# A four-layer graph network: late parameters by the loads' queue, masks in three stages, attention's input by quarters within the first loop, loops and slots by six places

## The chip, the cores and the metric

The kernel runs on one core of a Trainium2 chip. The metric is the device time of one execution in microseconds (us). The core's engines work side by side, each through its own instruction stream: TensorE (PE; its weight loads are listed apart as PEld), VectorE (DVE), ScalarE (ACT), GpSimd (POOL) and SyncE (SP), which here issues nearly all DMA transfers. The median before is 4793.08 us of three runs (4787.59 to 4794.63).

## The reference, cut to what matters

Eight samples of 2048 nodes with 128 features, one adjacency matrix of 2048 x 2048 shared by all, about 3% of it ones. Every layer normalises its input and applies relu, and its result is added to x.

```python
for layer in (0, 1, 2, 3):
    h = relu(layernorm(x))
    x = x + f[layer](h, adj)

# 0: h = layernorm(((w + 1) * h + b) @ W) * gamma + beta
#    e = leaky_relu(s1[i] + s2[j]); att = softmax(where(adj > 0, e, -9e15))
#    f = elu(att @ h + h)
# 1: four heads of 32: softmax(where(adj, q @ k.T / sqrt(32), -inf)) @ v @ Wo + bo
# 2: relu(h @ Wself + bself + (adj @ h / degree) @ Wneigh + bneigh)
# 3: h = h @ W.T; e = leaky_relu(s[i] + d[j]); f = softmax(where(adj, e, -1e9)) @ h
```

## The kernel before

**Tiles.** A sample's x lies in four chunks `xb[g]` of 128 x 4 x 128 (512 nodes each). Nodes go in 16 tiles of 128. The order of PE, DVE, ACT and POOL is the order in which Python emits the instructions; SP's order and the place of every tile in its pool are chosen by the framework. `later(f)` puts a reader of a PSUM tile off until more work has been issued, `settle` emits what was put off. `Steps.skewed(n, stages)` emits stage s of item i in step i + s, so that the items run through the stages one behind another; `merged` lays two lists side by side by weight.

**Parameters (L187 to L262).** All weight matrices and rows come by ACT's own DMA queue, nineteen transfers, in the order of the code: `w0`, seven more matrices (L200 to L206), five rows broadcast to 128 partitions, and then six small transfers into `rows` (node weights, node biases, the two attention vectors). `rows` is turned by PE (`pcol`) into columns which layer 0 needs.

**The head (L1142 to L1229).** `mask_steps` has one step per tile of 128 rows of adj: `one` loads 1 MB (L1144), compares into 0/1 (`nb01`, bf16, on DVE, L1146), raises it to the mask of attention (`pmt`, int8, with row sums, on ACT, L1149), stores it (L1152), transposes its 16 squares on PE in two halves of eight (L1162), copies one half into `mst` (fp8) by DVE (L1165) and one by ACT (L1167), and at the end of a group of three or two tiles stores `mst` to `mg_all` (L1169). `degrees` (L1176) computes reciprocal degrees and the bias rows of layer 2 (`hbs`, L1191). The first ten tiles are merged with `layer0_ahead(0)`, which prepares layer 0 of the first sample (load of h L587, normalise, `weigh` on POOL L592, transposes and projection, normalise, `scale` and `shift` on POOL L618 and L621). `gat_rows` then sends the row of s2 through memory, broadcast to all partitions. The other six tiles and `degrees` are merged into the first 35% of the first layer-0 loop, and `before_attention(0)` follows the loop.

**The loops of layers 0 and 3 (`gat_loop`, L452 ff.).** Nodes in six groups, `GROUPS`, of 3, 3, 3, 3, 2, 2 tiles. A step handles two tiles of neighbours jp: `leaky` (ACT, L508), `lowered` (DVE, L514), `exps` (ACT, L518), `masked` (DVE, L523), `product` (PE, L534, six or four times two matmuls into `gacc`). The stages of one step belong to different jp, one step apart. At the end of a group `ended` (L549) reads `gacc` and `closed` adds. `ahead(k + 1)` prepares the next group in between: `maxi` (`gat_maximum`, L445, DVE, reads a mask `pmg` of 256 KB loaded for it), `shifts` and `spread`, which sends the rows `ab` through memory by SP.

**Attention.** `before_attention(b)` (L682 ff.) normalises a chunk, turns it (L694), projects q and k (`pqk`) and v (`pv`), and stores them to memory, from where `heads` and `queries` load them. The 256 blocks (sample, 256 queries, head) run as a stream of sub-steps, twelve to a block, six to each half `t`: sub-step 0 issues `scores` (PE, L932), half of `values` and `exponentials` (ACT, L956) of the half before; 1 the other values; 2 `masked_scores` (DVE, L948); 3 and 4 the eight-fold transposes T0 and T1 of the block before (PE, L968); 4 and 5 the copies C0 and C1 (ACT, L973). `pending` carries the end of a group of four heads: `po`, `rT`, `pwo` and the addition to x.

**Laying the layers side by side.** While attention of sample b runs, layers 2 and 3 of sample b - 1 and layer 0 of sample b + 1 are laid between the sub-steps. `work` lays by weight. For samples 1 to 6 the loops are laid by `locked` instead: one loop step to three sub-steps. `PLACES` and `PLACES_B` say behind which of the three each stage goes, for the first half of the six sub-steps (A) and the second (B). In the last part of a sample `locked` also lays `tail` (`before_attention(b + 1)` and `layer0_ahead(b + 2)`) over the first 60% of the steps.

Of the kernel before, what the change touches and what calls it, by code (L numbers as in the profile page):

```python
# [31 lines left out]
def gnn_kernel(  # L32
# [94 lines left out]
    def later(f):  # L127
        unread.append([f])
        return unread[-1]
# [70 lines left out]
    wq = load_w("wq", W_q)  # L200
    wk = load_w("wk", W_k)
    wv = load_w("wv", W_v)
    wo = load_w("wo", W_o)
    wself = load_w("wself", W_self)
    wneigh = load_w("wneigh", W_neigh)
    w3 = load_w("w3", W3)  # L206
    gam = load_row("gam", ln_g)
    bet = load_row("bet", ln_b)
    bo1 = load_row("bo1", b_o)
    bself = load_row("bself", b_self)  # L210
    bneigh = load_row("bneigh", b_neigh)

    nc.vector.tensor_scalar(bo1, bo1, -1.0, None, ALU.add)
# [42 lines left out]
    pw3 = psum("pw3", (P, P))  # L256
    nc.tensor.transpose(pw3, w3, ident)
    nc.vector.tensor_copy(w3T[:, 0:P], pw3)

    pwa = psum("pwa", (P, 2))  # L260
    nc.tensor.matmul(pwa, w3, a12_3, start=True, stop=True)
    nc.vector.tensor_copy(w3T[:, P : P + 2], pwa)  # L262
# [318 lines left out]
    def layer0_ahead(b):  # L581
# [3 lines left out]
        def load(g):  # L585
            h[g] = new(hp3, "h", "h", (P, 4, P))
            nc.sync.dma_start(out=h[g], in_=x_chunk(b, g))  # L587

        def weigh(g):
            for k in range(4):  # L590
                t = 4 * g + k
                nc.gpsimd.tensor_scalar(  # L592
                    h[g][:, k, :], h[g][:, k, :], nw1[:, t : t + 1], nb[:, t : t + 1],
                    ALU.mult, ALU.add,
                )
# [21 lines left out]
        def scale(g):  # L617
            nc.gpsimd.tensor_tensor(hv(g), hv(g), bc_mid(gam, 4), ALU.mult)  # L618

        def shift(g):  # L620
            nc.gpsimd.tensor_tensor(hv(g), hv(g), bc_mid(bet, 4), ALU.add)  # L621
# [54 lines left out]
    def before_attention(b):  # L676
# [34 lines left out]
        def project_v(g):  # L711
# [16 lines left out]
        steps = Steps()  # L728
        steps.skewed(
            G,  # L730
            norm_stages(lambda g: xb[g], hdst) + [turned, project, project_v],
            1.0,
        )
        return steps
# [324 lines left out]
    SUB = 12  # L1059
    state = {"exp": None, "old": None, "older": None, "ahead": None, "pair": None, "ao": None}  # L1060

    def block_steps(n):
# [36 lines left out]

        def sub(t, s):  # L1100
            def go():
                if t == 0 and s == 0:
                    begin()
                old, older = state["old"], state["older"]
                if s == 0 and n < len(blocks):
                    scores(blk, t)
                if s < 2:
                    if t == 0 and real("older"):
                        values(older, 2 + s)
                    if t == 1 and real("old"):  # L1110
                        values(old, s)
                if s == 0 and state["exp"]:
                    exponentials(*state["exp"])
                    state["exp"] = None
                if s == 2 and n < len(blocks):
                    masked_scores(blk, t)
                    state["exp"] = (blk, t)
                if s in (3, 4) and real("old"):
                    turned(old, 2 * t + s - 3)
                if s in (4, 5) and real("old"):  # L1120
                    copied(old, 2 * t + s - 4)
# [15 lines left out]

    def mask_steps():
        steps = Steps()
        st = {}  # L1140

        def one(it):  # L1142
            at = new(ep, "e", "adj", (P, N), I32)
            nc.sync.dma_start(out=at, in_=adj[it * P : (it + 1) * P, :])  # L1144
            nb01 = new(op, "dump", "nb01", (P, N), BF16)
            nc.vector.tensor_scalar(nb01, at, 0.0, None, ALU.is_gt)  # L1146
            pmt = new(mp, "pm", "pmt", (P, N), I8)

            nc.scalar.activation(  # L1149
                pmt, nb01, AF.Copy, scale=-64.0, bias=64.0, accum_out=nsum[:, it : it + 1]  # L1150
            )
            nc.sync.dma_start(out=pm_all[it], in_=pmt)  # L1152
            gk = next(k for k, (i, n) in enumerate(GROUPS) if i <= it < i + n)
            i0, n = GROUPS[gk]
            if it == i0:
                st["m"] = new(ep, "e", "mst", (P, T, n * P), FP8)
            c = (it - i0) * P
            for g in range(T // 8):
                pt = psum("pmask", (P, 8, P), BF16)
                for k in range(8):  # L1160
                    jt = g * 8 + k
                    nc.tensor.transpose(pt[:, k, :], nb01[:, jt * P : (jt + 1) * P], ident_bf)  # L1162
                dst = st["m"][:, g * 8 : (g + 1) * 8, c : c + P]
                if g == 0:
                    nc.vector.tensor_copy(dst, pt, saturate=False)  # L1165
                else:
                    nc.scalar.copy(dst, pt, saturate=False)  # L1167
            if it == i0 + n - 1:
                nc.sync.dma_start(out=mg_all[gk], in_=st["m"])  # L1169

        for it in range(T):
            steps.add(5.0, lambda it=it: one(it))
# [45 lines left out]
    with tc.manual_schedule(engines=ENGINES):  # L1218
        st0, pre = layer0_ahead(0)
# [180 lines left out]
```

## Time and profile before

| what | value |
| --- | --- |
| median of three runs | 4793.08 us |
| profiled execution | 4792.7 us |
| its span, first to last instruction | 4790.8 us |
| PE busy | 4126.7 us, 86% |
| DVE busy | 3906.3 us, 82% |
| ACT busy | 3613.4 us, 75% |
| POOL busy | 454.9 us, 9% |
| mean granted clock of TensorE | 0.943 |
| moved by DMA | 423 MB, 88 GB/s over the span |

The page is one profiled execution. Busy shares are means over stages: in the row of slices each digit is the busy share of a fortieth of the span (120 us) in tenths, 9 being 90% or more, and PEclk the clock that TensorE was granted. A group line names line, engine, operation, destination and sources with their shapes and the count; behind the bars stand the busy sum in us and the mean of one in ns, then the idle time of the engine just before them and what ended most of it. A timeline line begins with the time from the start of the span and the duration. A line of waits names who waited, for whom, and sum in us, count and longest. Three groups fill much of the body: attention's copy of transposed tiles (ACT L973, 1007 us), its masked scores (DVE L948, 1212 us) and the loops' product (PE L534, 1122 us).

### The profile page before, as it was taken

How to read it: one execution, taken by the hardware profiler on the slowest of the kernel's cores; microseconds unless marked ns; L12 is line 12 of the kernel's file. 1: busy time of each engine (PE TensorE's matmuls, PEld its weight loads, DVE VectorE, ACT ScalarE, POOL GpSimd, SP SyncE). 2: the span in 40 equal slices, each digit the busy share in tenths (PEclk: the TensorE clock that was granted, in tenths of full speed). 3: DMA queues.
4: the chain of work that ended last, by engine and by line, in shares of the span. 5: the costliest groups of instructions: out<-in, count | busy, mean ns of one | idle time of the engine just before them, and what ended most of it. 6: DMA issues, size and time to landing. Idle time of an engine off the chain costs nothing.

```text
span 4790.8 us, 87729 instructions
## 1 busy us (share of the span) xinstructions
PE 4126.7 (86%) x33290; PEld 2842.0 (59%) x33290; DVE 3906.3 (82%) x8337; ACT 3613.4 (75%) x5121; POOL 454.9 (9%) x413
## 2 busy tenths in 40 slices
PE   2569998998898988998799988989889998989976
PEld 2535665576656666575665766567665666646645
DVE  5967777888978898788988889788987898658849
ACT  4637986698868988598885978689885988749926
POOL 2020002001200031001300012000310000000000
PEclk7768999999999999999999999999999999999988
DMA  8432113323232232412233132322324123222122
GB/s 268 137 91 57 46 40 114 95 59 102 79 123 62 68 103 76 133 51 86 82 103 102 59 101 77 120 66 68 103 74 134 50 73 99 79 77 61 52 89 76
DMA packets 308354, 423.34 MB, mean 88 GB/s; under 512 B 61222, under 2 KB 177628, under 8 KB 303836
## 3 DMA queue, kind: packets, MB, share of 16 engines
q1 hardware_dynamic: 305984, 416.85, 28.7%
q8 instruction: 263, 4.31, 0.4%
q14 instruction: 159, 1.30, 0.1%
q10 hardware_dynamic: 1948, 0.87, 0.1%
HBM read 365.78 MB, written 55.98 MB: 88 GB/s over the span
## 4 chain that ended last, share of the span: by engine, by line
PE 33%; DVE 29%; ACT 28%; issue 6%; DMA 3%; SPq 1%; ACTq 0%; DVEq 0%
ACT e L956 8%; ACT eT L973 8%; PE pt L968 7%; DVE e L948 7%; PE pagg L787 7%; PE gacc L534 6%; ACT ge L508 6%; PE sc L932 5%; DVE dump L445 4%; DVE ge L514 4%; DVE ge L523 4%; PE acc L983 3%; ACT ge L518 3%; PE ph L393 1%; DVE ln_s L336 1%
## 5 line engine op out<-in xcount | busy, mean ns | idle before, releaser
L973 ACT COPY eT<-pt 128x1024 f32<-128x1024 f32 x1024 | 1007.3, 1012 | 568.7 <-PE pt L968 566.0
L948 DVE CUSTOM_DVE_ANT_0 e<-sc,pm 128x1024 f32<-128x1024 f32 x1024 | 1211.5, 1220 | 212.0 <-PE sc L932 207.0
L534 PE MATMUL gacc<-haug,ge 128*128 128x129 f32 x8192 | 1122.4, 288 | 178.3 <-DVE ge L523 94.6
L968 PE MATMUL pt<-ident,e 128*128 128x128 f32 x8192 | 1079.0, 282 | 159.0 <-DVE amh L948 74.1
L534 PEld LDWEIGHTS gacc<-haug,ge 128*128 128x128 f32 x8192 | 1016.7, 199 | 335.5 <-issue 264.8
L968 PEld LDWEIGHTS pt<-ident,e 128*128 128x128 f32 x8192 | 943.5, 145 | 285.1 <-DVE amh L948 101.7
L956 ACT ACTIVATE e<-e,amn 128x2048 f32<-128x2048 f32 x512 | 1031.4, 2014 | 29.6 <-DVE amn L952 29.6
L508 ACT ACTIVATE ge<-ab,s 128x384 f32<-128x384 f32 (+1 forms) x1536 | 803.5, 577 | 121.5 <-DMA ab<-rowd 74.0
L932 PE MATMUL sc<-ks,qr 32*128 32x512 f32 x4096 | 786.9, 660 | 71.5 <-ACT eT L973 46.2
L514 DVE TENSOR_TENSOR ge<-ge,ab 128x768 f32<-128x768 f32 (+1 forms) x768 | 683.8, 890 | 52.5 <-ACT ge L508 46.2
L523 DVE SCALAR_TENSOR_TENSOR ge<-mg,ge 128x768 f32<-128x768 fp8e4 (+1 forms) x768 | 666.6, 868 | 24.7 <-ACT ge L518 23.2
L518 ACT ACTIVATE ge<-ge 128x768 f32<-128x768 f32 (+1 forms) x768 | 595.1, 776 | 118.0 <-DVE ge L514 115.9
L445 DVE CUSTOM_DVE_ANT_0 dump<-s2b,pmg 128x2048 bf16<-128x2048 f32 x256 | 585.5, 2287 | 39.4 <-DMA s2b<-rowd 32.2
L983 PE MATMUL acc<-eT,vv 128*32 128x256 f32 x8192 | 587.6, 397 | 2.6 <-ACT eT L973 2.6
L346 POOL TENSOR_TENSOR ln_r<-ln_ve,neg_half 128x4 f32<-128x4 f32 x160 | 207.2, 1295 | 3868.4 <-DVE ln_ve L340 3623.7
L983 PEld LDWEIGHTS acc<-eT,vv 128*32 128x32 f32 x8192 | 206.8, 111 | 508.7 <-issue 428.0
L932 PEld LDWEIGHTS sc<-ks,qr 32*128 32x128 f32 x4096 | 241.6, 189 | 263.9 <-ACT eT L973 142.5
L787 PE MATMUL pagg<-mt,hm 128*128 128x512 fp8e4 x1536 | 356.1, 381 | 9.3 <-DVE agT L805 9.3
L787 PEld LDWEIGHTS <-hm 128*128 128x128 bf16 x1536 | 147.2, 98 | 183.6 <-issue 30.7
L379 PE MATMUL ptr<-ident,h 128*128 128x128 f32 x512 | 92.3, 307 | 54.2 <-DVE amh L948 19.3
L1036 DVE TENSOR_TENSOR aoT<-po,rT 128x256 f32<-128x256 f32 x64 | 27.1, 424 | 127.6 <-ACT rT L1031 127.5
L379 PEld LDWEIGHTS ptr<-ident,h 128*128 128x128 f32 x512 | 66.8, 155 | 85.5 <-issue 28.8
(126 smaller groups left out, 2601.8 us busy)
## 6 DMA issues: line engine op xcount, KB each, us to landing
pmg<-pm_all SPq DMA_DIRECT2D x256, 256.0 KB
mg<-mg_all SPq DMA_DIRECT2D x128, 384.0 KB
pm<-pm_all SPq DMA_DIRECT2D x128, 256.0 KB
qr<-qd SPq DMA_DIRECT2D x1024, 32.0 KB
mt<-mt_all SPq DMA_DIRECT2D x64, 512.0 KB
ab<-rowd SPq DMA_DIRECT2D x64, 384.0 KB
adj<-in_adj_dram SPq DMA_DIRECT2D x16, 1024.0 KB
s2b<-rowd SPq DMA_DIRECT2D x16, 1024.0 KB
```

The costliest lines, as they stand in the source:

```text
L445: nc.vector.tensor_tensor_reduce(dump, st["s2b"], pm, UP, HIGHEST, ALU.add, ALU.min, st["mn"][:, it : it + 1])
L508: nc.scalar.activation(e[:, c, :], gr[k]["s1"], AF.Prelu, bias=st["s2"][:, j : j + 1], alpha=ALPHA)
L514: nc.vector.tensor_tensor(e, e, bc_mid(gr[k]["m"], 2), ALU.subtract)
L523: nc.vector.scalar_tensor_tensor(e, mt, BIG, e, ALU.mult, ALU.min)
L534: nc.tensor.matmul(gr[k]["acc"][:, q, :], e[:, c, q * P : (q + 1) * P], st["haug"][:, j, :], start=(j == 0 and q == 0), stop=(j == T - 1), ...
L787: nc.tensor.matmul(st["pa"], st["hm"][:, j, s, :], st["mt", g, j // 8][:, j % 8, :], start=(j == 0 and s == 0), stop=(j == T - 1 and s == ...
L932: nc.tensor.matmul(blk["sc"][g // 2][:, (g % 2) * 512 : (g % 2 + 1) * 512], blk["q"][r, t * P : (t + 1) * P], ks_t[b, hh][r, :], start=Tru ...
L948: nc.vector.tensor_tensor_reduce(e[:, c], blk["sc"][h], pm[:, c], UP, HIGHEST, ALU.add, ALU.min, mh[:, h : h + 1])
L956: nc.scalar.activation(blk["e"][t], blk["e"][t], AF.Exp, scale=-1.0, bias=blk["mn"][:, t : t + 1], accum_out=blk["ao"]["sum"][:, t, blk["h ...
L968: nc.tensor.transpose(pt[:, c, t, :], blk["e"][t][:, j * P : (j + 1) * P], ident)
L973: nc.scalar.copy(eT, blk.pop(("pt", w)).rearrange("p c t n -> p c (t n)"))
L983: nc.tensor.matmul(pair["acc"][g * HD : (g + 1) * HD, blk["hh"] % 2, :], vv_t[blk["b"], blk["hh"]][:, j, :], blk["eT"][w][:, g, :], start= ...
```

## The change

Parameters: ten of the thirteen matrices and rows are issued by SP, behind four loads of h and four of adj. What is computed of `w3` and `bo1` moves to `late_constants`, which runs behind `gat_rows`.

Masks: the step of a tile is split into three stages that run skewed, with the loads of adj four tiles ahead. The transposes of a tile go into one PSUM tile and ACT copies it whole; DVE copies none. `mst` and `nb01` take slots of other pools. Eleven entries of the skewed list are merged with layer 0's preparation, three more run before the loop, the rest (last stores and `degrees`) in its first tenth. `weigh`, `scale` and `shift` of sample 0 run on DVE.

Attention's input: `before_attention` can be emitted for some of the four chunks. For sample 0 chunk g goes into the loop, one step of it per loop step, once group 1, 2, 3 or 5 has closed.

Loops and slots: `ORDER` lists what each of the six sub-steps emits; T1 moves from sub-step 4 to 3. `locked` has six places to a loop step instead of three, one before and one behind each of the three sub-steps (odd ones are behind: 1, 3, 5 are the old 0, 1, 2). `product` goes from the second to the third sub-step, `maxi` of the second half from behind the second to before the first, `ended` of the first half from the second to the first. The share of `tail` falls from 0.6 to 0.55.

```diff
-    wq = load_w("wq", W_q)
...
-    bneigh = load_row("bneigh", b_neigh)
-
-    nc.vector.tensor_scalar(bo1, bo1, -1.0, None, ALU.add)
+    late = [("wq", W_q), ("wk", W_k), ("wv", W_v), ("wo", W_o), ("wself", W_self)]
+    late += [("wneigh", W_neigh), ("w3", W3), ("bo1", b_o), ("bself", b_self), ("bneigh", b_neigh)]
...
+    def load_late():
+        for t, ap in late.values():
+            nc.sync.dma_start(out=t, in_=ap if len(ap.shape) == 2 else ap.partition_broadcast(P))
...
-    def layer0_ahead(b):
+    def layer0_ahead(b, eng=nc.gpsimd):
...
+    ORDER = [
+        ["S", "V0", "exp"],
+        ["V1"],
+        ["ttr"],
+        ["T0", "T1"],
+        ["C0"],
+        ["C1"],
+    ]
...
+    def neighbours(it):
+
+        nb01[it] = new(tp, "eT", "nb01", (P, N), BF16)
+        nc.vector.tensor_scalar(nb01[it], adj_t.pop(it), 0.0, None, ALU.is_gt)
+        load_adj(it + 4)
+
+    def mask_turned(it):
+        gk, i0, n = group_of(it)
+        if not mst:
+            mst["all"] = new(bp, "big", "mst", (P, 2, T, 3 * P), FP8)
+        mst[gk] = mst["all"][:, gk % 2, :, 0 : n * P]
+        c = (it - i0) * P
+        pt = psum("pmask", (P, T, P), BF16)
+        for jt in range(T):
+            nc.tensor.transpose(pt[:, jt, :], nb01[it][:, jt * P : (jt + 1) * P], ident_bf)
+        later(lambda: nc.scalar.copy(mst[gk][:, :, c : c + P], pt, saturate=False))
...
+        steps.skewed(T, [neighbours, turned_raised, mask_stored], 5.0)
...
-        early, late = Steps(masks_all[:10]), Steps(masks_all[10:])
-        rest = merged(early, pre)
-        rest.add(1.0, lambda: gat_rows(st0))
-        rest.extend(merged(layer0_loop(0, st0, True), late, 0.35))
-        rest.extend(before_attention(0))
+        n = 11
+        rest = merged(pre, Steps(masks_all[:n]))
+        rest.add(1.0, lambda: gat_rows(st0), lambda: load_x(0))
+        rest.add(1.0, late_constants)
         run(rest)
+        loop = layer0_loop(0, st0, True)
+        quarters, queue, others = before_attention(0), [], masks_all[n:]
+        start = len(loop) - 9 * len(GROUPS) - 6
+        for _ in range(3):
+            run([others.pop(0)])
...
+            for g, group in enumerate((1, 2, 3, 5)):
+                if k == start + 9 * group + 13:
+                    queue.extend(quarters([g]))
+            if queue:
+                run([queue.pop(0)])
+        run(others + queue)
...
-        PLACES = {'product': 1, 'masked': 0, 'exps': 1, 'lowered': 0, 'leaky': 1, 'ended': 1, 'closed': 0, 'maxi': 0, 'other': 2}
-        PLACES_B = {'product': 1, 'masked': 0, 'exps': 0, 'lowered': 1, 'leaky': 0, 'ended': 1, 'closed': 1, 'maxi': 1, 'other': 2}
+        PLACES_A = {
+            "product": 5, "masked": 1, "exps": 3, "lowered": 1, "leaky": 3,
+            "ended": 1, "closed": 1, "maxi": 1, "other": 5,
+        }
+        PLACES_B = {
+            "product": 5, "masked": 1, "exps": 1, "lowered": 3, "leaky": 1,
+            "ended": 3, "closed": 3, "maxi": 0, "other": 5,
+        }
...
-                    locked(both[n:], tail, 0.6)
+                    locked(both[n:], tail, 0.55)
```

## The prediction

> **What bounds the kernel now.** I read the slices first, then the busy time by stage, then the timeline at the ends of the stages, then the groups and waits inside them.
>
> ```profile
> PE   2569998998898988998799988989889998989976
> DVE  5967777888978898788988889788987898658849
> ACT  4637986698868988598885978689885988749926
> PEclk7768999999999999999999999999999999999988
> ```
> A slice is 120 us. The first three slices show PE at 2, 5 and 6 tenths, and DVE and ACT hardly better: nothing is full there. From the fourth on PE stands at 8 or 9, ACT and DVE close behind, and the three change places as the fullest. So the kernel has a head that waits and a long body that is packed. The change touches both.
>
> The head by stages (columns: stretch, us, busy of PE, PEld, DVE, ACT, POOL with counts, clock, DMA share, GB/s), and one stretch of the body for comparison:
>
> ```profile
> 0.00:97.30 97.30, 26.89 (x217) 23.33 (x217) 48.67 (x149) 40.92 (x55) 31.36 (x46) 0.83 0.81 273
> 97.30:117.70 20.40, 3.78 (x32) 3.25 (x32) 14.37 (x16) 5.86 (x7) 0.00 (x0) 0.50 0.78 246
> 117.70:258.30 140.60, 84.33 (x577) 78.30 (x577) 131.31 (x223) 94.22 (x162) 0.00 (x0) 0.80 0.42 131
> 258.30:287.20 28.90, 19.54 (x72) 11.83 (x72) 11.80 (x62) 8.43 (x16) 10.15 (x9) 0.74 0.49 152
> 2212.00:2401.00 189.00, 151.96 (x1228) 109.87 (x1228) 173.85 (x398) 147.80 (x216) 53.28 (x41) 0.94 0.30 89
> ```
> Masks and projections (0 to 97.3) have no engine above half and DMA at 81%: the chain adj, compare, transposes, two copies, store runs nearly one tile after the other. The first layer-0 loop (117.7 to 258.3) has DVE busy 93%: DVE is its pace. In the 28.9 us before the first attention block every engine is under 70%: a chain of dependent steps. The last row, seventeen half-blocks in which attention's next input is laid beside the loop, has DVE at 92%; 15.1 us of it are idle.
>
> ```profile
> 15.33 1.28 ACT L1149 ACT_TABLE_LOAD   x1 [15.33 <-DMA rows<-in_L_gnn_node_bias_dram]
> 117.66 2.13 ACT L508 ACTIVATE ge<-ab,s 128x384 f32<-128x384 f32 x4 [5.12 <-DMA ab<-rowd]
> 287.23 1.23 DVE L948 CUSTOM_DVE_ANT_0 e<-sc,pm 128x1024 f32<-128x1024 f32 x1 [11.78 <-PE sc L932]
> ```
> Start, duration, and in brackets the wait with its releaser: ACT's first work, the first step of the loop, the first masked scores. All further numbers are counted to these three.
>
> **The change part by part.** The sum is made against the profiled execution: 4792.7 us, span 4790.8, which is within 0.4 us of the median of the runs (4793.08), so no correction is needed.
>
> *Parameters.* ACT's first work waits for a row that was queued behind the ten parameters. Ten issues of about 0.45 us leave ACT (4.5), and SP takes them after four h and four adj loads. Here the Trainium skill, "DMA: Bandwidth & Descriptors", section on issuing engines not being separate DMA queues, speaks against more: several issuers share the 16 engines and save issue time only. By that rule 4.5 us at most are won, no transfer time. The trace's row lets ACT start 15.3 late with DMA at 81%, which agrees; I take 3.3, start near 12, as the small rows now also land beside the h and adj loads.
>
> *Masks in three stages.*
> ```profile
> L1165 DVE CAST mst<-pmask x16: 1224/1225/1225, 23.3 to 160.9; 128x1024 fp8e4<-128x1024 bf16 x16
> L1167 ACT CAST mst<-pmask x16: 987/1012/1012, 24.1 to 161.8; 128x1024 fp8e4<-128x1024 bf16 x16
> ```
> Two half copies per tile, DVE 1.225 and ACT 1.01, become one ACT copy of twice the width. "ScalarE: Activation LUTs", section Rules for kernel authors, gives such simple work to VectorE, up to three times faster in bf16. By the rule DVE should have kept both halves, and the move would cost 16 times at least 1.2 us on ACT for nothing. The row says ACT is faster on this copy, 1.01 to 1.225, so I follow the row: one ACT copy at 1.9 (between one 1.01 and two of them, less one fixed start; upper end 2.02). ACT then carries per tile 1.91 (raise) + 0.19 (sum) + 1.9 = 4.0, times 16 = 64, and 11.3 for layer 0's projections, about 5 of gaps: from 12 to 92. DVE and POOL are relieved (weigh, scale and shift of sample 0 go from POOL to DVE, which has room: 48.7 of 97.3). Then the rows of s2, the first maxima and the shifts: 20.4 us now; the next three mask tiles lie beside it, and the maxima's loads stand on SP behind the stores of masks 11 to 13. I let the loop begin at **104** (was 117.66). Bounds: DMA must move some 31 MB before it (16.8 adj, 8.4 mask stores, 5.5 h, x, parameters and rows), 283 GB/s is the best 60 us I read: 110; without that limit 98. Gain 13.7 (6 to 20).
>
> *The first loop.*
> ```profile
> L1165 DVE CAST mst<-pmask 128x1024 fp8e4<-128x1024 bf16 x4 | 4.9, 1225 | 3.8 <-PE pmask L1162 3.8
> L1146 DVE TENSOR_SCALAR nb<-adj 128x2048 bf16<-128x2048 int32 x4 | 4.9, 1220 | 0.0
> L1191 DVE SCALAR_TENSOR_TENSOR hbs<-bneigh,has,bself 128x128 f32<-128x128 f32 x16 | 4.3, 332 | 0.0
> ```
> These are DVE's mask groups inside the loop: count, busy and mean ns, then idle before and its releaser. They leave it: 4.9 + 4.9 + 3.8 of waiting + 4.3 and 0.7 of small steps = 18.6. Three quarters of before_attention come in: DVE's statistics and normalising, about 2.5 each (0.86 + 0.36 + 0.17 + 1.1) = 7.5. DVE is the pace, so 140.6 - 11.1 = **129.5**: the loop ends at 233. ACT rises from 94 by three turns and projections, about 12, still under 129; that hides it. If ACT's copies stood between two leaky steps on the path, 5 come back.
>
> *Input by quarters.* After the loop, 28.9 us now: four skewed quarters and the loads of q, k, v. One quarter stays: statistics 1.6, root 1.0 on POOL, apply 1.1, turn 2, projection 2, copies 2, two DMA trips of about 2 to 3 and the scores 2.6: about 17. First masked scores at **250** (was 287.2); so far 37. From 287 to 340 the first blocks have waits of up to 15 us; k, v and the second sample's h come earlier, I take 3. Head: **-40** (20 if the early stage is bound by DMA and the quarters delay the loop, 52 if neither).
>
> *Loops by six places.* In steady halves the order of PE and ACT stays; what changes is below.
> ```profile
> PE gacc L534 <- DVE x L881: 55.0, 21, 5.7
> PE pt L968 <- ACT eT L973: 36.7, 5, 7.3
> ```
> Sum, count and longest, from 750 to 4092. The first: PE's first product of a layer-3 group waits for `ended`, which stood on DVE behind `masked` and `lowered` (0.95 each). It goes ahead of both, so up to 1.9 of each wait goes, 21 x 1.9 = 40. About half of these stretches are DVE's, where PE's wait costs nothing: -18. The second: `T0` and `T1` fell into one PSUM bank, five times, T1 waiting 7.3 for a copy. With T1 one sub-step earlier they have different banks; that stretch (2363.2 to 2378.6) has DVE busy 15.16 of 15.4, so DVE is late next and I count 0 (bound 36). What queues behind T1 on PE is the older work, `pv`, `pwo`, which now comes after both: their readers on DVE and ACT come up to 1.1 later, cost 0 to 1 per place.
>
> Tail 0.6 to 0.55: 26 steps in 29.7 instead of 32.4 loop steps. The same DVE and POOL work in a denser stretch; 2.7 steps of half a half-block (8.8: some 560 us of a sample over 64) at some tenths of loss: **+6** for six samples (0 to 12), given back in part by looser steps behind.
>
> `maxi` now stands on DVE ahead of `masked` in every second half:
> ```profile
> L445 DVE CUSTOM_DVE_ANT_0 dump<-s2b,pmg 128x2048 bf16<-128x2048 f32 x256 | 585.5, 2287 | 39.4 <-DMA s2b<-rowd 32.2
> ```
> Ten of a loop's sixteen fall there, 60 in six samples. Below, it can gain: `masked_scores` behind it comes up to 0.4 sooner after the last copy, 24. Above, if `masked` is late for PE by all of 2.29, 137. The row it is nearest to is `masked` itself, whose product PE takes only in the following half-block, over 7 us later, so I take **0**. In samples 0 and 7 the loops are laid by weight and not by places; there only T1 moves: -3.
>
> Body: -18 + 0 + 6 + 0 - 3, rounded to **-12** for what the looser steps return or take (-40 to +25). Ceiling of any gain on DVE: 15.1 idle in each of six tails, 90. Sum: 4792.7 - 40 - 12 = 4741.
>
> **The rivals.**
> A: only the head gains. For it: DVE is at 92% or more wherever loops run, so an earlier `ended` merely moves DVE's order, and the denser tail costs its 6 to 12. Against it: 55 us of PE waiting are on one cause, and PE is at 9 tenths in many slices. Time: 4792.7 - 35 + 5 = about 4763.
> B: the body gains its bounds: 40 from L881, 24 from the maxima, less 6, with the head's 40: 4792.7 - 98 = about 4695. For it: three engines are so close that any wait may be on the path. Against it: the gains would all have to fall where PE or ACT is the pace.
> C: the early stage is DMA's, at 81% already, the parameters only change places, SP's queue holds up `ab` of the first group behind dv_all and two hb_all stores: the loop begins at 114, loses 5 more to late loads and ends at 249; first masked scores at 266, the head gives 21 and the body nothing: about 4772.
> D, the other side: `maxi` ahead of `masked` is exposed on PE. Place: every second half of layer 3's loop; price up to 2.29, sixty times. The gains above, 52, are used up once 0.87 us of each is exposed; at full exposure 4741 + 137 = 4878. For it: DVE has the fewest gaps there (15.16 of 15.4 us busy), so no gap swallows an operation put ahead. Against it: DVE does no more than before, and the product waits one half-block later anyway.
> E, that the change does not do what it says: the mask stages would show no overlap if the two buffers for 0/1 tiles, shared with attention's transposed tiles, held the skew to one. Two buffers suffice for compare beside turn, so this has little weight and its time is C's.
>
> **How the numbers follow.** Forecast (head 30 to 50, body -30 to +5: 4715 to 4768) 0.62, A beyond that 0.14, B 0.12, C and E 0.07, D 0.05. Predicted 4741. The range 4700 to 4773 takes in A, C and half of B; left out are the rest of B and D, about one in ten, and misjudged sizes another. A measurement of this kernel tells 0.2%, 9.6 us, from no change. Faster by more, below 4783.5: all but D and a sliver of C, 0.92; within 0.03; slower 0.05.
>
> **What would show each step.** ACT's first work near 12 and the pm store of the sixteenth mask near 92 (parameters, masks); first leaky near 104 with its wait on `ab` at most 5; the loop 129 to 130 long with DVE above 93% and no mask group in it; first masked scores near 250. In the body: PE's sum on L881 down to 40 or less, the 7.3 on the copy of L973 gone, the mean of a half-block in samples 1 to 5 at 8.8 or a little less. I am wrong in the head if ACT's copy of 128x2048 takes over 2.1, or DMA stands above 85% up to the loop and it begins after 112; wrong in the body if PE's waits on L523 grow by more than 20 us (D), or if L881's wait falls and the half-block stays (A).

## The result and the profile after

The changed kernel takes 4715.05 us, median of four runs (4711.7 to 4723.47), against 4793.85 for the kernel before beside it: a ratio of 0.9841, 95% interval 0.9824 to 0.9858. The profiled execution took 4711.7, its span 4709.8. So 79 us went, by the spans 81.0; forecast were 52.

Where they went, from the start of ACT's exponentials (the first of each sample's, from the timeline):

| stretch | before | after | difference | forecast |
| --- | --- | --- | --- | --- |
| start to first leaky step | 117.7 | 110.1 | -7.6 | -13.7 |
| to first masked scores | 169.6 | 147.0 | -22.6 | -23 |
| to first exponential | 9.7 | 10.4 | +0.7 | |
| sample 0 | 456.5 | 448.1 | -8.4 | -4.5 |
| samples 1 to 6 | 3344.5 | 3315.2 | -29.3 | -12 |
| sample 7, to the last exponential | 459.6 | 449.0 | -10.6 | -1.5 |
| last exponential to the end | 233.3 | 230.2 | -3.1 | 0 |

Each stretch is read from one profiled execution of each kernel. In the forecast column the 3 us of T1 are shared by samples 0 and 7, and the head's 3 us for the first blocks stand in sample 0; the column adds up to 55, since the prediction rounded its body from 15 to 12. The head gave some 30 us, less than the 40 forecast, and the body 51, four times the 12 forecast. The two misses partly cancel in the sum.

The slices of the page, after the change (each 118 us):

```profile
PE   3669998998899988999899988999889998989966
DVE  5967767888978988788988889788887899758849
ACT  6639985798849888598876988589884998849926
```

ACT's first slice rises from 4 tenths to 6, PE's first two from 2 and 5 to 3 and 6; the body looks the same. The answers to the windows and the timeline show more (columns as in the prediction):

```profile
8.00:99.00 91.00, 37.08 (x313) 32.30 (x313) 54.59 (x175) 69.17 (x73) 12.03 (x9) 0.70 0.88 318
99.00:110.00 11.00, 0.37 (x1) 0.09 (x1) 7.63 (x26) 1.74 (x1) 0.00 (x0) 0.50 0.76 245
110.00:242.80 132.80, 89.30 (x560) 80.92 (x560) 125.33 (x226) 88.69 (x161) 23.34 (x6) 0.78 0.57 159
242.80:257.00 14.20, 8.09 (x22) 4.37 (x22) 5.54 (x29) 2.67 (x5) 3.29 (x3) 0.64 0.39 120
```
```profile
8.05 1.28 ACT L1193 ACT_TABLE_LOAD   x1 [8.05 <-DMA rows<-_L_gnn_node_weights_dram]
13.92 1.91 ACT L1193 ACTIVATE pmt<-nb 128x2048 int8<-128x2048 bf16 x1 [4.58 <-DVE nb L1176]
110.05 1.12 ACT L508 ACTIVATE ge<-ab,s 128x384 f32<-128x384 f32 x2 [9.31 <-DMA ab<-rowd]
242.84 0.17 DVE L549 RECIPROCAL grec<-gacc 128x2 f32<-128x2 f32 x1 [2.28 <-PE gacc L534]
257.03 1.23 DVE L957 CUSTOM_DVE_ANT_0 e<-sc,pm 128x1024 f32<-128x1024 f32 x1 [6.77 <-PE sc L941]
```

Two lines of the kernel before belong beside these, its first raised mask and the last read of the first loop's sums:

```profile
16.62 1.91 ACT L1149 ACTIVATE pmt<-nb 128x2048 int8<-128x2048 bf16 x1
256.10 0.17 DVE L549 RECIPROCAL grec<-gacc 128x2 f32<-128x2 f32 x1 [1.44 <-PE gacc L534]
```

ACT's first instruction, a table load, comes 7.3 us sooner, but ACT then waits 4.58 for DVE's first compare: the first mask is raised at 13.9 instead of 16.6, only 2.7 sooner. The masks now have a DMA share of 0.88 at 318 GB/s, and ACT is busy 69.2 of 91: transfers are the fullest resource of that stage, and only half of the forecast gain came. From its first leaky step to the last read of its sums the first loop takes 132.8, with DVE busy 94% of it, instead of 138.4, and 14.2 us follow instead of 31.1. (The prediction's 140.6 and 28.9 count the loop to its last addition to x, some 2 us later.)

The waits of PE over samples 1 to 6 (sum, count, longest), to be laid beside the two lines of before in the prediction:

```profile
PE pt L977 <- DVE amh L957: 151.7, 87, 5.9
...
PE gacc L534 <- DVE x L890: 15.6, 5, 3.1
...
```

The wait on DVE x went from 55.0 to 15.6; the wait of T1 on the copy, 36.7 before, is 6.9 (L977 on L982). The wait on `amh` (the transposes waiting until DVE has read the score tiles) more than doubled, from 66.5: PE now waits for DVE at another place. From 735 to 4010 us PE is busy 90% of the time, DVE 87% and ACT 80%: no engine bounds this region alone, and sums of PE's waits don't tell how much a change gained.

### The profile page after: what moved, and what is told of

It reads as the page before. It is cut to its first block, busy times and chain, and to the rows that moved or that the text cites. A ratio compares the mean times of both kernels' runs of the same rounds, so it can differ in the third digit from the quotient of the medians.

```text
span 4709.8 us, 87633 instructions
## 1 busy us (share of the span) xinstructions
PE 4100.3 (87%) x33290; PEld 2831.7 (60%) x33290; DVE 3876.3 (82%) x8345; ACT 3622.3 (77%) x5121; POOL 470.3 (10%) x389
## 4 chain that ended last, share of the span: by engine, by line
DVE 32%; PE 32%; ACT 25%; issue 6%; DMA 5%; SPq 1%; POOL 0%; ACTq 0%; DVEq 0%; POOLq 0%
DVE e L957 9%; ACT e L965 7%; PE pagg L796 7%; ACT eT L982 7%; PE pt L977 6%; PE gacc L534 6%; ACT ge L508 5%; DVE dump L445 5%; PE sc L941 5%; DVE ge L514 4%; DVE ge L523 4%; PE acc L992 3%; ACT ge L518 3%; DMA ab<-rowd 2%; DVE ln_s L336 1%
## 5 line engine op out<-in xcount | busy, mean ns | idle before, releaser
L982 ACT COPY eT<-pt 128x1024 f32<-128x1024 f32 x1024 | 999.7, 1015 | 482.4 <-PE pt L977 480.3
L977 PE MATMUL pt<-ident,e 128*128 128x128 f32 x8192 | 1057.4, 281 | 203.2 <-DVE amh L957 163.1
L977 PEld LDWEIGHTS pt<-ident,e 128*128 128x128 f32 x8192 | 934.8, 145 | 320.3 <-DVE amh L957 198.6
L508 ACT ACTIVATE ge<-ab,s 128x384 f32<-128x384 f32 (+1 forms) x1536 | 805.4, 579 | 110.1 <-DMA ab<-rowd 85.9
L941 PE MATMUL sc<-ks,qr 32*128 32x512 f32 x4096 | 770.7, 661 | 67.1 <-ACT eT L982 47.0
L518 ACT ACTIVATE ge<-ge 128x768 f32<-128x768 f32 (+1 forms) x768 | 597.6, 779 | 147.9 <-DVE ge L514 147.0
L514 DVE TENSOR_TENSOR ge<-ge,ab 128x768 f32<-128x768 f32 (+1 forms) x768 | 666.9, 868 | 44.4 <-ACT ge L508 40.3
L346 POOL TENSOR_TENSOR ln_r<-ln_ve,neg_half 128x4 f32<-128x4 f32 x160 | 218.9, 1368 | 3847.8 <-DVE ln_ve L340 3598.9
L1008 ACT COPY oT<-acc 128x512 f32<-128x512 f32 x128 | 74.8, 585 | 55.0 <-PE acc L992 55.0
```

What stands on the lines that cost most here:

```text
L508: nc.scalar.activation(e[:, c, :], gr[k]["s1"], AF.Prelu, bias=st["s2"][:, j : j + 1], alpha=ALPHA)
L514: nc.vector.tensor_tensor(e, e, bc_mid(gr[k]["m"], 2), ALU.subtract)
L941: nc.tensor.matmul(blk["sc"][g // 2][:, (g % 2) * 512 : (g % 2 + 1) * 512], blk["q"][r, t * P : (t + 1) * P], ks_t[b, hh][r, :], start=Tru ...
L977: nc.tensor.transpose(pt[:, c, t, :], blk["e"][t][:, j * P : (j + 1) * P], ident)
L982: nc.scalar.copy(eT, blk.pop(("pt", w)).rearrange("p c t n -> p c (t n)"))
```

## The experiments

r1 to r10 put one or more things back into the changed kernel; r11 and r12 change it further. Names of lines are those of the changed kernel. Time of a sample is measured as in the table above; DVE busy comes from the windows view over samples 1 to 6. "Slow" counts the steps of `lowered` (L514) there that took over 1.3 us instead of 0.95 or 0.69. The runs of r4, r5, r6, r9, r10 and r12 overlap with the changed kernel's own (4711.7 to 4723.47), so a difference of less than some 10 us from it is not clear of the noise; what is said of such a run rests on its trace, one execution.

| kernel | median us | ratio to before, 95% | samples 1-6 | DVE busy | slow | samples 0 + 7 |
| --- | --- | --- | --- | --- | --- | --- |
| before | 4793.85 | | 3344.5 | 2884.2 | 20 | 916.1 |
| after | 4715.05 | 0.9824-0.9858 | 3315.2 | 2865.7 | 3 | 897.1 |
| r1 old body | 4758.8 | 0.9915-0.9954 | 3351.6 | 2884.7 | 18 | 912.0 |
| r2 T1 back | 4742.6 | 0.9881-0.9919 | 3337.0 | 2864.3 | 3 | 911.9 |
| r3 places back | 4748.8 | 0.9898-0.9931 | 3349.8 | 2887.8 | 20 | 901.7 |
| r5 `ended` back | 4722.9 | 0.9843-0.9874 | 3325.6 | 2864.0 | 1 | 898.0 |
| r6 `product` back | 4721.5 | 0.9840-0.9870 | 3323.2 | 2866.9 | 5 | 900.2 |
| r7 `maxi` back | 4727.7 | 0.9853-0.9882 | 3327.9 | 2873.3 | 9 | 901.2 |
| r8 share back | 4700.2 | 0.9794-0.9829 | 3303.4 | 2873.3 | 9 | 897.3 |

### Head or body, T1 or places

**r1, the changed head with the body of before**

```diff
-        ["T0", "T1"],
-        ["C0"],
+        ["T0"],
+        ["T1", "C0"],
...
-            "ended": 1, "closed": 1, "maxi": 1, "other": 5,
+            "ended": 3, "closed": 1, "maxi": 1, "other": 5,
...
-            "ended": 3, "closed": 3, "maxi": 0, "other": 5,
+            "ended": 3, "closed": 3, "maxi": 3, "other": 5,
...
-                    locked(both[n:], tail, 0.55)
+                    locked(both[n:], tail, 0.6)
```
with "product" 3 instead of 5 in both halves.

> The changed kernel with the body of before: T1 in sub-step 4, the loops' places as before, tail share 0.6. Only the head is new. Theory (the head is worth what the first exponential shows, 296.9 to 267.4): 4793.9 - 29.5 = about 4764, first masked scores at 257, samples 0 to 7 from the first exponential on as long as before within 1 us each. Rival (the head's earlier loads also shorten sample 0 behind its first block, which is 8.4 us shorter in the changed kernel): about 4756.

Measured: 4758.8, first masked scores at 258.7, sample 0 back at 455.1. The head alone is worth about 29 us by the span (4761.7) and 34 by the medians; the rival's shorter sample 0 did not come with it. The other samples differ from before's by up to 2.7 us either way, more than the 1 that was expected. The other 52 (spans) or 44 (medians) are the body's.

**r2, T1 alone back in sub-step 4** (the first part of the diff above)

> The changed kernel with T1 alone back in sub-step 4. Theory A (the body's gain is largely T1's: samples 0 and 7, whose loops are not laid by places, lost 8.4 and 10.7 us, and samples 1 to 6 some 2 each): 4715 + 30 = about 4745, samples 0 and 7 back to 456.5 and 459.6. Theory B, the prediction's (T1 gives 3, the places the rest): about 4718, samples 0 and 7 within 3 us of the changed kernel's.

Measured: 4742.6, samples 0 and 7 together 911.9 as with the old body: theory A. The 3 us that the prediction gave T1 are refuted. One half-block of sample 7 shows the mechanism; first with T1 back, then as changed (timeline: start, duration, engine and line, in brackets the wait and who ended it):

```profile
4336.49 1.09 PE L977 MATMUL pt<-ident,e 128*128 128x128 f32 x8 [0.55 <-DVE aoT L1045]
4338.49 0.71 PE L1050 MATMUL pwo<-wo,aoT 128*128 128x128 f32 x4 [0.92 <-DVE amh L957]
4339.64 1.09 PE L977 MATMUL pt<-ident,e 128*128 128x128 f32 x8 [0.43 <-DVE amh L957]
...
4340.83 1.01 ACT L982 COPY eT<-pt 128x1024 f32<-128x1024 f32 x1 [2.14 <-PE pt L977]
```
```profile
4303.55 1.09 PE L977 MATMUL pt<-ident,e 128*128 128x128 f32 x8 [0.55 <-DVE aoT L1045]
4305.56 1.09 PE L977 MATMUL pt<-ident,e 128*128 128x128 f32 x8 [0.92 <-DVE amh L957]
4306.71 0.71 PE L1050 MATMUL pwo<-wo,aoT 128*128 128x128 f32 x4
...
4306.75 1.01 ACT L982 COPY eT<-pt 128x1024 f32<-128x1024 f32 x1 [1.00 <-PE pt L977]
```

With T1 late, `pwo` stands between T0 and T1, takes the first score tile that DVE gives free, and T1 waits for the second. ACT waits 2.14 for T1's tile, 1.00 with T1 early, and the exponentials behind that copy start 1.1 sooner. ACT is on the path here, not DVE, which had been idle for 4.6 us just before. `pwo` comes in eight half-blocks of a sample. In sample 7 these eight (2, 10, 18 and so on to 58, counted from 0) are 0.5 to 1.2 us shorter each, together 8.1 of the sample's 8.8; with the old places (r1 against r3) the same eight give 8.0. The group lines of this copy, before and after, give the sum of ACT's idle time in front of it over the whole kernel:

```profile
L973 ACT COPY eT<-pt 128x1024 f32<-128x1024 f32 x1024 | 1007.3, 1012 | 568.7 <-PE pt L968 566.0
...
L982 ACT COPY eT<-pt 128x1024 f32<-128x1024 f32 x1024 | 999.7, 1015 | 482.4 <-PE pt L977 480.3
```

It is 563.0 in r2, 571.7 in r1 and 508.2 in r3, so 63 to 81 us of ACT's waiting go with T1, whatever the places are. This too is a sum of waits and not a time.

**r3, places and share back, T1 early** (the other parts of r1's diff)

> The changed kernel with the loops' places and the share of 0.6 as before, T1 early as in the change. Theory A (places are worth what T1 leaves of the body's 51, some 22): about 4737, PE's wait of L534 on DVE x L890 back from 15.6 to about 55. Theory B (the places are the body's main gain, 40 or more): about 4757. Rival C (the places and T1 only gain together, because T1's earlier slot makes room that the moved product fills): 4760 or more here and in the run with T1 back alike.

Measured: 4748.8, in between. Four spans make the table of two factors: neither 4761.7, places alone 4747.8 (r2), T1 alone 4748.0 (r3), both 4709.8. Each alone gives 14, both 52: the rival C's kind of case, gains that come together, though both runs lie 11 to 17 us under the 4760 that it named. By the medians the two give 16 and 10 alone and 44 together, so the excess is some 18 to 24 us. Most of it lies in samples 1 to 6: places alone 14.6, T1 alone 1.8, both 36.4. "Places" here takes in the share of the tail, which r8 takes apart. The columns of the table tell two things apart there. DVE busy falls by 20 to 22 with the places, with T1 or without; DVE's idle time is 466.9 (r1), 472.7 (r2), 462.0 (r3) and 449.5 (after). So the places shorten DVE's own work, and the earlier T1 seems to turn into time only once DVE is less full. The first of these is traced below; the second fits the runs and was not shown step by step.

### The places one by one

**r5, `ended` of the first half at its old place**

```diff
-            "ended": 1, "closed": 1, "maxi": 1, "other": 5,
+            "ended": 3, "closed": 1, "maxi": 1, "other": 5,
```

> The changed kernel with `ended` of the first half back at its old place (behind the second sub-step, after `masked` and `lowered`); all else as changed. Theory (the prediction's term: the first product of a layer-3 group waits 1.9 less): PE's wait of L534 on DVE x L890 back from 15.6 to 50 or more, 4715 + 18 = 4733. Rival (with product behind the third sub-step, `ended` comes early enough anyway): the wait stays under 25, 4717.

Measured: 4722.9, +8 (samples 1 to 6: +10.4). PE's waits:

```profile
PE gacc L534 <- DVE x L890: 30.8, 20, 4.9
```

The wait comes back to 30.8, not 50: of the 39 us that the change took off it, this place accounts for 15. What they were worth in time is the 8 to 10 above, at the edge of the noise. With everything but `product` changed (r6) the sum stays 15.6, with all places old (r3) it is 58.0.

**r6, `product` behind the second sub-step again**

```diff
-            "product": 5, "masked": 1, "exps": 3, "lowered": 1, "leaky": 3,
+            "product": 3, "masked": 1, "exps": 3, "lowered": 1, "leaky": 3,
...
-            "product": 5, "masked": 1, "exps": 1, "lowered": 3, "leaky": 1,
+            "product": 3, "masked": 1, "exps": 1, "lowered": 3, "leaky": 1,
```

> The changed kernel with `product` back behind the second sub-step. Theory (the product behind T0 and T1 gives PE's matmuls for attention first, which T1's early slot needs; places and T1 gain 24 only together): 4715 + 24 = about 4739, and PE's wait of T1 on the copy of L982 comes back to about 36. Rival (the product's place costs and gains nothing, as the prediction had it): 4715.

Measured: 4721.5, samples 1 to 6 +8.0, and T1's wait on the copy stays at 6.9. The theory is refuted. The rival's 4715 is not: the 6 to 8 us lie within the noise.

**r7, `maxi` of the second half behind the second sub-step again**

```diff
-            "ended": 3, "closed": 3, "maxi": 0, "other": 5,
+            "ended": 3, "closed": 3, "maxi": 3, "other": 5,
```

> The changed kernel with `maxi` of the second half back behind the second sub-step. Theory (the prediction's: 0): 4715 within 4. Rival A (maxi ahead of `masked` lets the rows `ab` of the next group leave sooner): 4725, with ACT's wait of L508 on DMA ab longer than 46.6. Rival B (maxi ahead costs PE what `masked` is late): 4705, with ACT's wait of L518 on L514 back from 101.6 to about 70.

Measured: 4727.7, +12.6, samples 1 to 6 +12.7; the wait on the rows `ab` is 43.8, not longer than 46.6, so rival A has the time nearly right and the mechanism wrong; rival B is refuted by the time and by ACT's wait of L518, 109.0 instead of about 70. DVE's busy time is what moved, by 7.6 of the 12.7: 2873.3 against 2865.7. The same stretch of sample 3, with `maxi` back:

```profile
2207.81 2.29 DVE L445 CUSTOM_DVE_ANT_0 dump<-s2b,pmg 128x2048 bf16<-128x2048 f32 x1
2210.03 0.09 DVE L445 DVE_READ_ACCUMULATOR2_ANT mn<- 128x1 f32 x1
2210.03 2.02 DVE L514 TENSOR_TENSOR ge<-ge,ab 128x768 f32<-128x768 f32 x1
...
2207.99 3.25 POOL L697 TENSOR_TENSOR x<-x,bo 128x512 f32<-128x512 f32 x1 [0.23 <-DVE h L353]
```
and as changed:
```profile
2193.92 2.28 DVE L445 CUSTOM_DVE_ANT_0 dump<-s2b,pmg 128x2048 bf16<-128x2048 f32 x1
...
2198.03 0.95 DVE L514 TENSOR_TENSOR ge<-ge,ab 128x768 f32<-128x768 f32 x1
...
2194.16 2.92 POOL L346 TENSOR_TENSOR ln_r<-ln_ve,neg_half 128x4 f32<-128x4 f32 x1 [2.54 <-DVE ln_ve L340]
```

POOL's addition of x and bo (1.27 when nothing is beside it) was issued while `maxi` ran, took 3.25, and the `lowered` step that follows `maxi` took 2.02 instead of 0.95: it paid for POOL's operation. With `maxi` put ahead, it covers POOL's root operation instead, which takes 2.92 instead of 1.0 and holds nobody up. Every slow step of the table's rows before (20), after (3) and r7 (9) is of this kind: an operation of POOL over a whole tile (this addition, or layer 0's shift, L624 in the changed kernel) began earlier and ends 1.1 to 1.2 us after the step begins. Six of r7's nine are additions issued while `maxi` ran. The group lines of `lowered` before and after, both from 740 to 4050 us, show the sum:

```profile
L514 DVE TENSOR_TENSOR ge<-ge,ab 128x768 f32<-128x768 f32 x382 | 384.1, 1005 | 28.3 <-ACT ge L508 27.8
```
```profile
L514 DVE TENSOR_TENSOR ge<-ge,ab 128x768 f32<-128x768 f32 x384 | 369.1, 961 | 24.6 <-ACT ge L508 24.2
```

15 us of DVE, from twenty such collisions to three. That is most of the 18.5 us that DVE's busy time lost. With `maxi` back six of the 17 collisions that went return, with the share back (r8, below) as many; the rest was not taken apart.

**r8, the tail's share 0.6 again**

```diff
-                    locked(both[n:], tail, 0.55)
+                    locked(both[n:], tail, 0.6)
```

> The changed kernel with the tail's share back at 0.6. Theory (the prediction's: the denser tail costs 6): 4709, half-blocks 44, 49 and 54 of samples 2 to 5 (counted from 0), 2.6 to 4 us longer in the changed kernel than with the old places, back to their old lengths. Rival (the denser tail ends sooner, and what is free behind it returns more, the 6.4 us of half-block 56): 4715 + 12 = 4727.

Measured: 4700.2, 15 us faster than the changed kernel, the four runs of each apart (4694.8 to 4705.4 and 4711.7 to 4723.5). The sign of the prediction's term was right and its size too small. Half-blocks 44, 48, 49 and 54 of samples 2 to 5 are 1.8 to 3.9 us shorter, while 56 is 3.5 longer; slow steps and T1's wait on the copy are back (37.5, eleven times), and the kernel is faster all the same. So that wait does not decide over the time, and it is not T1's place that decides over the wait but the share: r8 differs from the changed kernel by the share alone, r2 has T1 at its old place, the new share and only 4.7 of this wait, r3 has T1 early, the old share and 35.5.

### The head

**r4, attention's input wholly behind the first loop**

```diff
-            for g, group in enumerate((1, 2, 3, 5)):
-                if k == start + 9 * group + 13:
-                    queue.extend(quarters([g]))
-            if queue:
-                run([queue.pop(0)])
-        run(others + queue)
+        run(others + quarters(range(G)))
```

> The changed kernel with attention's input of sample 0 wholly behind the first loop again. Theory (DVE is the loop's pace, so the loop gets shorter by the 7.5 us of three quarters and the stretch behind it longer, from 14.2 to 28.9): first masked scores at 257 + 7 = 264, time 4715 + 7 = 4722. Rival (the quarters fill DVE's and ACT's gaps and cost the loop nothing): first masked scores at 271, time 4730.

Measured: 4719.6, first masked scores at 262.8. The loop (first leaky step to the last read of its sums) takes 122 instead of 133, so the quarters cost it 11, forecast 7.5; they save 17 behind it. The theory holds in the trace; the gain of this part is some 5 us, within the noise of the medians.

**r9, the mask's copy split between DVE and ACT again**

```diff
-        later(lambda: nc.scalar.copy(mst[gk][:, :, c : c + P], pt, saturate=False))
+        def read():
+            nc.vector.tensor_copy(mst[gk][:, 0:8, c : c + P], pt[:, 0:8, :], saturate=False)
+            nc.scalar.copy(mst[gk][:, 8:16, c : c + P], pt[:, 8:16, :], saturate=False)
+
+        later(read)
```

> The changed kernel with the mask's copy split again: eight squares by DVE, eight by ACT, from the same PSUM tile. Theory (transfers pace the head: from 8 to 99 us the DMA share is 0.88 at 318 GB/s, ACT busy only 69.2 of 91): first leaky step at 110 within 2, time 4715 within 5. Rival (ACT paces the masks, 4.0 us to a tile; the split takes 0.86 of it): the first eleven tiles 9 us sooner, first leaky step at 101 to 104, time 4707.

Measured: 4720.7, first leaky step at 115.6: both theories miss. Relieving ACT (busy 52.4 of 91 instead of 69.2) brought nothing, so ACT was not the pace; but the first maxima came at 92.5, 97.0 and 101.5 instead of 89.8, 93.1 and 96.5. The first of them waits for a transfer, in both kernels, and why that lands 2.7 later was not traced; each of the other two loses 1.1 to 1.2 more, since it now stands on DVE behind a copy of 1.22 as well as a compare. The whole copy on ACT takes 1.862 (1.9 in the prediction), and it pays at least by what it takes off DVE there.

**r10, the ten parameters issued by ACT first**

```diff
+    for t, ap in late.values():
+        nc.scalar.dma_start(out=t, in_=ap if len(ap.shape) == 2 else ap.partition_broadcast(P))
...
-        load_late()
```

> The changed kernel with the ten parameters issued by ACT ahead of the small rows again, not by SP. Theory (issue time of ACT is 4.5, the transfers are the same, and the head is paced by them): ACT's table load at 13 to 15 instead of 8, but the first leaky step at 110 to 113, time 4715 + 2. Rival (the late start goes through to the end of the head): first leaky step at 116, time 4721.

Measured (timeline, ACT's issues and its first work):

```profile
2.63 0.86 ACTq L207 DMA_DIRECT2D wk<-in_L_gnn_W_k_dram  x1
4.12 0.33 ACTq L207 DMA_DIRECT2D wv<-in_L_gnn_W_v_dram  x1
6.51 0.33 ACTq L207 DMA_DIRECT2D wo<-in_L_gnn_W_o_dram  x1
7.49 0.33 ACTq L207 DMA_DIRECT2D wself<-in_L_gnn_W_self_dram  x1
...
18.05 1.28 ACT L1195 ACT_TABLE_LOAD   x1 [18.05 <-DMA rows<-_L_gnn_node_weights_dram]
19.34 1.91 ACT L1195 ACTIVATE pmt<-nb 128x2048 int8<-128x2048 bf16 x1
```

The issues are short, but gaps of 0.6 to 2.1 us lie between them, in which ACT issues nothing: ten parameters put the table load off by 10.0 us, not by the 4.5 of their issue times. What fills the gaps was not traced. Since ACT waits for DVE's compare in the changed kernel, the first mask is raised only 5.4 later (19.34 against 13.92), and that goes through to the end of the head: the first leaky step is at 115.2, 5.1 later, as the rival had it. First masked scores are 4.4 later; the span is 3.7 longer, and the median, 4715.7, is within the noise of the changed kernel's, where the theory had it.

**r11, x loaded in the first loop, share 0.6**

```diff
-        rest.add(1.0, lambda: gat_rows(st0), lambda: load_x(0))
+        rest.add(1.0, lambda: gat_rows(st0))
...
             run([step])
+            if k == start:
+                load_x(0)
...
-                    locked(both[n:], tail, 0.55)
+                    locked(both[n:], tail, 0.6)
```

> The changed kernel with the share at 0.6 and the four loads of x of the first sample issued in the first loop instead of behind the first rows (SP took from 70.5 to 76.5 to get past three of them, and only then issued s2b). Theory (the queue's order holds the first maxima up): first maximum at 84 instead of 89.8, first leaky step at 104, time 4700 - 6 = 4694. Rival (only the bytes count, 1.05 MB at 318 GB/s): first leaky step at 107, time 4697. Rival B (the x loads now stand in front of the loop's own small loads): 4700 or more.

In the changed kernel SP's queue reads (timeline, issues only):

```profile
68.33 1.86 SPq L403 DMA_DIRECT2D rowd<-row  x4
70.54 2.92 SPq L162 DMA_DIRECT2D x<-in_x_dram  x3
76.55 0.34 SPq L406 DMA_DIRECT2D s2b<-rowd  x1
```

Measured: with x gone from there, s2b is still issued at 77.0, the first maximum comes at 87.2, not 84, and the first leaky step at 107.6; nine profiles with the changed kernel's early stage have it at 109.2 to 112.2, and r12, early stage as here, at 108.8. That is the bytes' share, the rival, if it is anything: the time, 4697.7, can't be told from r8's 4700.2. It is the fastest version measured (0.9789 to 0.9818 of before), by r8's edit above all.

**r12, r11 with the share at 0.65**

```diff
-                    locked(both[n:], tail, 0.6)
+                    locked(both[n:], tail, 0.65)
```

> The changed kernel with late x loads as in the run before and the tail's share at 0.65. Theory (the tail's DVE and POOL work costs less the thinner it lies; 0.55 to 0.6 gave 12 to 15): about 4697.7 - 10 = 4688, samples 2 to 5 some 2 us each below 551. Rival (at 0.6 the gain is used up, since it came from where single steps fall and not from their density): 4698 within 4. Rival B (the tail now runs into the next sample's start, whose first half-blocks wait for q, k and v): above 4702, with the first two half-blocks of samples 2 to 6 longer.

Measured: 4719.7. None of the three as it stands: thinner is not faster, the gain at 0.6 is lost again, and the first half-blocks of a sample are not what got longer; 47, 52 and 57 did, by 2.0, 5.6 and 2.9. Of the 23 us between the spans of r11 and r12 only 13 lie in samples 1 to 6; 8 lie in the head and behind the last exponential, where the two kernels do the same. The gain does not follow density; that it comes from where single steps fall fits these runs and was not traced.

## Why the prediction came out as it did

- **Parameters and masks** (start at 12, loop at 104). ACT's table load came at 8, but its first mask only 2.7 sooner than before, near the 3.3 that were counted; put back whole (r10), the ten parameters delay that mask by 5.4, a little more than the 4.5 of issue time that the prediction took as the most to win. The loop began at 110, the end that was named for a stage bound by DMA. r9 shows that ACT's 4.0 us to a tile were not the pace. The term was mis-sized: 7.6 instead of 13.7, because the sum paced the stage by ACT. That transfers pace it instead is likely, by their share of 0.88 and r11, where 1.05 MB less brought the first maximum 2.6 sooner (at 318 GB/s they would take 3.3, an estimate), and not shown. ACT's copy of the mask has the size that was forecast: 1.86, against two halves of 1.22 and 1.01.
- **The first loop and the quarters** (the loop 11.1 shorter, the stretch behind it 11.9). Counted from the same marks, the loop became 5.6 shorter and the stretch behind it 16.9: the terms are off by 5.5 and 5.0, in opposite directions, and only the sum is right. r4 takes the first apart: without the quarters the loop is 16.3 shorter (18.6 were forecast), and they cost it 10.7 rather than 7.5. The 3 us for the first blocks behind it did not come: with the old body sample 0 is only 1.4 shorter.
- **`ended`** (-18). The mechanism was right, the size not: 8 to 10 from this place (r5), and 15 of the 39 us that PE's wait lost.
- **T1** (-3). This step failed. The prediction looked at it as a matter of banks and of PE's waits, found DVE late next, and overlooked ACT's idle time in front of the copy, 568.7 us on the page of before. It did see that `pwo` falls behind T1, but counted only what `pwo`'s readers lose, 0 to 1 per place, and not the 1.1 that T1's copy gains there. r2 and r3 give T1 10 to 15 in samples 0 and 7 alone, and 14 to 38 in the whole kernel. The wait of 36.7 that it hoped to remove did go, but with the share (r8): there the sign that was named came true by luck.
- **`maxi` and `product`** (0 each). `maxi` failed as well, with 13; the 6 of `product` are within the noise. For `maxi` the prediction asked who waits for `masked`, and did not ask which DVE operation stands beside POOL's. Its rival D, that `maxi` ahead of `masked` is exposed, is refuted by r7. Rival A is refuted too, and B, the body gaining its bounds, came nearest for the body: it had it at -58 and the head at -40. But it had 40 of the 58 from `ended` and nothing from T1, so its size is in part luck.
- **The tail's share** (+6). Right in sign, 12 to 15 in size. The reason given, that a denser tail costs, does not hold beyond 0.6 (r12).

The forecast's direction held. The time lies within the range in part by luck: the head's shortfall of 10 stood against a body that gave 39 more, most of it from terms put at 3 or at nothing. (One sum of the prediction is off: the lower end of its forecast, head -50 and body -30, is 4713, not 4715.)

## What to carry to other kernels

Where three engines are nearly full, look at the idle time in front of every large group on each of them, not only at the waits of the engine that is busiest; the same edit can be worth nothing alone and 20 us with another. When an operation moves in a hand-written order, ask what runs on the neighbouring engine at that moment. And undo a change part by part even when it is a gain: here one part, the share, took back 15 of what the others gave.

## What the runs showed of the hardware

DVE's `lowered` (two f32 inputs in SBUF) and POOL's addition over 128x512 hold each other up. Behind an addition that had waited for `maxi`, `lowered` takes 2.02 instead of 0.95; with `maxi` on DVE it is POOL's operation that waits (the root, 2.92 instead of 1.0), and `maxi` keeps its 2.29. Which of the two waits does not follow from who was issued first alone. Five times in samples 1 to 6 of the changed kernel the addition is issued while `masked` runs, 0.7 ahead of `lowered`, and it is the addition that waits:

```profile
2208.52 0.95 DVE L523 SCALAR_TENSOR_TENSOR ge<-mg,ge 128x768 f32<-128x768 fp8e4 x1
2209.39 0.95 DVE L514 TENSOR_TENSOR ge<-ge,ab 128x768 f32<-128x768 f32 x1
...
2208.69 2.80 POOL L697 TENSOR_TENSOR x<-x,bo 128x512 f32<-128x512 f32 x1 [4.34 <-DVE h L353]
```

So where an operation that is long and is not held up, as `maxi` here, is placed decides what is held up beside it. The Trainium skill, "GPSIMD Engine Reference", section Specifications, says that POOL's SBUF interfaces are shared with VectorE, with contention for instructions of two SBUF inputs; the lines above agree and show what it costs here.
